# Starting expert 0 of a mixture of experts inside the routing that feeds it

## The chip, the cores and the metric

The kernel runs on one core of a Trainium2 chip. The metric is the device time of one launch, in microseconds (us); lower is better. Engines are named as in the profile: PE (TensorE matmul), PEld (its weight loads), DVE (VectorE), ACT (ScalarE), POOL (GpSimd) and SP (SyncE); the q after a name is that engine's queue of instructions.

## What is computed

A graph attention network of two layers on 1250 nodes of 768 features, then a transformer block: attention over the 1250 rows, and a mixture of experts with 8 experts, of which each row uses 2. The change concerns the last part, in the reference:

```python
logits = xf @ Wrouter                                   # (1250, 768) @ (768, 8)
topk_w, topk_idx = jax.lax.top_k(logits, 2)
topk_w = softmax(topk_w)
we = zeros((N, E)).at[arange(N)[:, None], topk_idx].add(topk_w)
...
h = gelu(xf @ W1e)                                      # 768 -> 384, for each expert e
acc = acc + we_e[:, None] * (h @ W2e)                   # 384 -> 768
```

and the block returns x + attention + that sum, where xf is the layer norm of x + attention. Everything is in 32-bit floats.

## The kernel before

Rows are worked on in 10 row tiles of T = 125 rows. `product(t)` (line 878) multiplies a row tile of the attention result by the output projection (`po`, 12 matmuls of 384 columns, 24 rows in the profile[...]), adds the residual and normalises twice (lines 886 to 892), and sends x + attention to `out` in DRAM from SP or ACT (line 893). The normalised rows are `yn`, one of three buffers.

`route(t, yn, seen)` (line 896) transposes yn on PE (`ptr`, line 140), evicts it through ACT with the norm's scale and bias (`fT`, line 146), multiplies by the router (`pl`, line 901, 8 columns), takes the two largest logits and their indices on DVE, makes one-hot rows `oh`, and counts on PE how many earlier rows chose the same expert (`prk`, lines 918 and 920; `seen` carries the counts of earlier tiles). That count is the row's place among its expert's rows; the slot is 1280 times the expert plus the place (line 939). The two softmax weights are computed with Exp and a reciprocal (lines 927 to 934). Two indirect DMAs from POOL then scatter the row, with four words behind its 768 (row number, first expert, the two weights; RW = 772), into the DRAM table `xd` (line 941). The loop of lines 952 to 957 issues product(t + 1) ahead of route(t); within each engine a scheduler orders the instructions.

After the last tile, `pn` (line 961) counts the rows of each expert over all tiles. From it DVE finds which experts have more than CAP = 384 rows (`used`, `more`, lines 963 to 966) and where the first spare tile is (`pick`, lines 825 to 834). Every engine loads `more` into a register, SP loads the place as well, and a loop (line 1050) runs for each further spare tile; with the given inputs it runs zero times. At the end of such a loop all engines and DMA queues meet.

Experts are worked on as a list of `jobs` (line 1061): expert 0 to 7 with 384 slots, that is three slot tiles of 128 rows, and one spare tile. For each job, `fetch` reads slot tiles from `xd` on SP (`xr`, line 988), `turn` transposes them on PE (`pt`, 6 times 3 transposes) and evicts them through ACT (`xT`), `first` (line 1019) is 18 matmuls (`phe`, 36 rows in the profile) with Gelu on ACT (`hT`), `second` (line 1029) is 6 matmuls for each slot tile (`poe`, 12 rows in the profile), whose result DVE weighs and adds to what the row has so far (`sofar`). `tokens` (line 991) makes the ids and weights on DVE, `results` (line 1003) gathers `sofar` from `out`, and `second` scatters it back; gathers and scatters are indirect DMAs from POOL, ordered job after job because two experts can share a row. The weights of the next expert, `we`, are loaded by SP into one of two buffers while the present one runs, ahead of the next rows; those of expert 0, `first_w`, are loaded early in routing.

The order of the DMAs that SP issues once the loop is passed is: expert 0's three tiles of xr, expert 1's two weight matrices, its three tiles, expert 2's weights, and so on:

```python
xr = fetch(xd[0:CAP, :], NS)
...
over = nc.values_load(more[0:1, 0:1], min_val=0, max_val=NE * NR)
with tc.For_i(0, over, 1):
```

Of the kernel before, what the change touches and what calls it, by code (L numbers as in the profile page):

```python
# [27 lines left out]
def gnn_ffn_kernel(  # L28
# [49 lines left out]
    RW = D + 4  # L78
# [786 lines left out]

    with tc.tile_pool(name="proj", bufs=3, reuse_waits="tile") as pp, \
            tc.tile_pool(name="ppo", bufs=2, space=PSUM) as ppo, \
# [5 lines left out]

        normed = [pp.tile([P, RW], F32, tag=f"yn{i}", name=f"yn{i}", bufs=1) for i in range(3)]
# [3 lines left out]
        def product(t):  # L878
            po = ppo.tile([T, 2, 512], F32, tag="po", name="po")
            for s in range(2):  # L880
                for c in range(DC):
                    nc.tensor.matmul(po[:, s, :DH], aT[:, c, t * T:(t + 1) * T],  # L882
                                     wp[:, c, s * DH:(s + 1) * DH],
                                     start=(c == 0), stop=(c == DC - 1))
            y2 = pp.tile([T, D], F32, tag="y2", name="y2")
            ln_apply(y2, xs[:, t, :], st0[:, 0, t:t + 1], st0[:, 1, t:t + 1])
            o = y2.rearrange("p (s d) -> p s d", s=2)
            nc.vector.tensor_tensor(o, o, po[:, :, :DH], ALU.add)
            mean, rstd = ln_stats(y2)
            yn = normed[t % len(normed)]  # L890
            ln_apply(yn[:T, :D], y2, mean, rstd)
            nc.vector.tensor_add(xs[:, t, :], xs[:, t, :], y2)
            split_rows(nc.sync if t % 2 == 0 else nc.scalar, out[t * T:(t + 1) * T, :], xs[:, t, :])
            return yn

        def route(t, yn, seen):
            fT = pp.tile([P, DC, T], F32, tag="fT", name="fT", bufs=2)
            transpose_rows(ppt, yn[:T, :D], affine(fT, 0, 2))
            pl = ppl.tile([P, 512], F32, tag="pl", name="pl")
            for c in range(DC):  # L900
                nc.tensor.matmul(pl[:T, :NE], fT[:, c, :], wr[:, c, :],
                                 start=(c == 0), stop=(c == DC - 1))
            lg = small.tile([T, NE], F32, tag="lg", name="lg")
# [12 lines left out]
            nc.vector.tensor_add(both, oh[:, 0, :], oh[:, 1, :])  # L916
            pr = ppl.tile([P, 512], F32, tag="pl", name="prk")
# [8 lines left out]

            ex = small.tile([T, 2], F32, tag="ex", name="ex")
            nc.vector.tensor_sub(ex[:, 0:1], top[:, 1:2], top[:, 0:1])
            nc.scalar.activation(ex[:, 0:1], ex[:, 0:1], AF.Exp)
            nc.vector.tensor_scalar(ex[:, 1:2], ex[:, 0:1], 1.0, None, ALU.add)  # L930
            nc.vector.tensor_copy(yn[:T, D:D + 1], number[:, t:t + 1])
            nc.vector.tensor_copy(yn[:T, D + 1:D + 2], atf[:, 0:1])
            nc.vector.reciprocal(yn[:T, D + 2:D + 3], ex[:, 1:2])
            nc.vector.tensor_mul(yn[:T, D + 3:D + 4], ex[:, 0:1], yn[:T, D + 2:D + 3])
# [10 lines left out]
            return new  # L945
# [6 lines left out]
        yns = [product(0)]  # L952
        seen = None
        for t in range(NT):
            if t + 1 < NT:
                yns.append(product(t + 1))
            seen = route(t, yns[t], seen)
# [17 lines left out]
    with tc.tile_pool(name="moe", bufs=2, reuse_waits="tile") as mp, \  # L975
# [15 lines left out]
        def tokens(xr, e, n, tag):  # L991

            ids = mp.tile([P, NS], I32, tag=tag + "ids", name="ids")
            nc.vector.tensor_copy(ids[:, :n], xr[:, :n, D])
            weight = mp.tile([P, NS], F32, tag=tag + "weight", name="weight")
            part = mp.tile([P, NS], F32, tag=tag + "part", name="part")
            nc.vector.tensor_sub(part[:, :n], xr[:, :n, D + 2], xr[:, :n, D + 3])
            nc.vector.scalar_tensor_tensor(part[:, :n], xr[:, :n, D + 1], e, part[:, :n],
                                           op0=ALU.is_equal, op1=ALU.mult)
            nc.vector.tensor_add(weight[:, :n], part[:, :n], xr[:, :n, D + 3])  # L1000
            return ids, weight

        def results(ids, s, row):
            nc.gpsimd.indirect_dma_start(
                out=row, out_offset=None, in_=out,
                in_offset=bass.IndirectOffsetOnAxis(ap=ids[:, s:s + 1], axis=0),
                bounds_check=N - 1, oob_is_err=False)

        def turn(xr, n):
            xT = mp.tile([P, DC, CAP], F32, tag="xT", name="xT")  # L1010
            for c in range(DC):
                pt = mpt.tile([P, 512], F32, tag="pt", name="pt")
                for s in range(n):
                    nc.tensor.transpose(pt[:, s * P:(s + 1) * P], xr[:, s, c * P:(c + 1) * P], ident)
                nc.scalar.activation(xT[:, c, :n * P], pt[:, :n * P], AF.Identity,
                                     scale=lnp[:, 2, c:c + 1], bias=lnp[:, 3, c:c + 1])
            return xT

        def first(w1, xT, n):
            hT = mp.tile([P, FC, CAP], F32, tag="hT", name="hT")  # L1020
            for f in range(FC):
                ph = mph.tile([P, 512], F32, tag="ph", name="phe")
                for c in range(DC):
                    nc.tensor.matmul(ph[:, :n * P], w1[:, c, f * P:(f + 1) * P], xT[:, c, :n * P],  # L1024
                                     start=(c == 0), stop=(c == DC - 1))
                nc.scalar.activation(hT[:, f, :n * P], ph[:, :n * P], AF.Gelu)
            return hT

        def second(w2, hT, s, ids, weight, row):
            po = mpo.tile([P, 2, 512], F32, tag="po", name="poe")  # L1030
            for d in range(2):
                for f in range(FC):
                    nc.tensor.matmul(po[:, d, :DH], hT[:, f, s * P:(s + 1) * P],  # L1033
                                     w2[:, f, d * DH:(d + 1) * DH],
                                     start=(f == 0), stop=(f == FC - 1))
            o = row.rearrange("p (s d) -> p s d", s=2)
            nc.vector.scalar_tensor_tensor(o, po[:, :, :DH], weight[:, s:s + 1], o, op0=ALU.mult, op1=ALU.add)  # L1037
            nc.gpsimd.indirect_dma_start(
                out=out, out_offset=bass.IndirectOffsetOnAxis(ap=ids[:, s:s + 1], axis=0),
                in_=row, in_offset=None, bounds_check=N - 1, oob_is_err=False)  # L1040

        xr = fetch(xd[0:CAP, :], NS)
# [7 lines left out]
        with tc.For_i(0, over, 1):  # L1050
# [5 lines left out]
            ids, weight = tokens(xo, picked[:, EXTRA, 0:1], 1, "o")  # L1056
            results(ids, 0, sofar[0])
            second(w2, first(w1, turn(xo, 1), 1), 0, ids, weight, sofar[0])

        extra = [place(i) for i in range(EXTRA)]  # L1060
        jobs = [(float(e), NS, expert(e), lambda e=e: xd[e * REG:e * REG + CAP, :]) for e in range(NE)]
        jobs += [(picked[:, i, 0:1], 1, chosen(e), lambda r=r: xd[ds(r, P), :])
                 for i, (e, r) in enumerate(extra)]
        xT = turn(xr, NS)
        for i, (e, n, _, _) in enumerate(jobs):
            w1, w2 = w
            hT = first(w1, xT, n)
            ids, weight = tokens(xr, e, n, "")
# [3 lines left out]
            if i + 1 < len(jobs):  # L1072
# [3 lines left out]
                xT = turn(xr, m)  # L1076
# [33 lines left out]
```

## Time and profile before

| | us |
|---|---|
| median of 3 runs | 1528.72 |
| lowest and highest | 1525.68, 1529.65 |
| time of the profiled run | 1527.86 |
| its span, first to last instruction | 1526.1 |
| mean granted clock of PE | 0.961 |
| PE busy | 1442.0 (94%) |
| DVE, ACT, POOL busy | 813.5, 598.0, 433.7 |

By stage, from the windows of the trace (busy us of each engine, and the granted clock of PE as a share of full speed):

| stage | from, to | PE | DVE | ACT | POOL | PE clock |
|---|---|---|---|---|---|---|
| graph, attention | 0, 1184 | 1125.2 | 711.8 | 502.7 | 356.3 | 0.72 to 1.00 |
| projection and routing | 1184, 1276 | 92.0 | 61.3 | 41.0 | 22.7 | 1.00 |
| hand-over to the experts | 1276, 1300 | 8.6 | 9.6 | 8.9 | 3.9 | 0.62 |
| expert 0, into expert 1 | 1300, 1346 | 43.6 | 5.0 | 11.9 | 9.2 | 0.90 |
| experts | 1346, 1526 | 172.6 | 25.9 | 33.4 | 41.6 | 0.99 |

A busy share says how long an engine had work in flight; a stage's length is set by the engine or wait that the chain runs through. In a list of instructions, the bracket after a row is the idle time before it on its engine and what ended it. A tile's name stands for its buffers.

### The profile page before, as it was taken

The page shows a single profiled execution, that of the slowest core. Times are in us where ns is not written, and L with a number is a line of the kernel's source. Part 1 is how long each engine was busy: PE and PEld are TensorE (multiplying, and loading weights), DVE is VectorE, ACT ScalarE, POOL GpSimd, SP SyncE. Part 2 cuts the span into 40 slices and gives each one's busy share as a digit, 9 for nine tenths or more (in the row PEclk, how much of TensorE's full clock was granted, in tenths as well). Part 3 has the DMA queues.
Part 4 walks back from the last instruction along what each step waited for, and adds up shares of the span by engine and source line. Part 5 has one row for each costly group of instructions (what it writes and reads, how often), then busy time and mean ns, then how long its engine had stood idle before and what let it go on. Part 6 is the DMA issues. An engine that isn't in the chain of part 4 may idle for free.

```text
span 1526.1 us, 15935 instructions
## 1 busy us (share of the span) xinstructions
PE 1442.0 (94%) x5957; PEld 781.8 (51%) x5957; DVE 813.5 (53%) x1326; ACT 598.0 (39%) x949; POOL 433.7 (28%) x288
## 2 busy tenths in 40 slices
PE   5699999999999999999999999999989996899998
PEld 3476655556555555553343343344333664566665
DVE  4797655435036650128778778778787764111111
ACT  3321613205116521236646646646656344221211
POOL 6300000000000010006646656655657222122222
PEclk9856999999999999999999999999999997899999
DMA  7100010000031129920000000000120433855644
GB/s 216 33 2 12 11 73 0 1 19 14 0 103 41 61 82 395 407 100 1 21 0 1 21 1 21 1 21 1 29 73 1 143 112 113 299 169 174 223 152 143
DMA packets 48848, 125.50 MB, mean 82 GB/s; under 512 B 6103, under 2 KB 22680, under 8 KB 48768
## 3 DMA queue, kind: packets, MB, share of 16 engines
q1 hardware_dynamic: 30958, 55.99, 11.0%
q0 software_dynamic: 12688, 57.10, 10.0%
q10 hardware_dynamic: 5122, 11.36, 2.6%
q8 instruction: 48, 0.79, 0.2%
q14 instruction: 32, 0.26, 0.1%
HBM read 71.30 MB, written 57.60 MB: 84 GB/s over the span
## 4 chain that ended last, share of the span: by engine, by line
PE 71%; DVE 9%; issue 8%; DMA 6%; ACT 4%; POOL 1%; POOLq 0%; SPq 0%; ACTq 0%; DVEq 0%
PE pagg L542 12%; PE ph L209 9%; PE st L694 8%; PE pav L738 7%; PE pk L657 5%; PE pv L673 5%; PE phe L1024 5%; PE poe L1033 5%; PE pq L657 4%; PE pc L419 2%; DMA xd<-yn,slot 2%; DVE sT L724 2%; PE po L882 2%; ACT sT L697 1%; DVE most L703 1%
## 5 line engine op out<-in xcount | busy, mean ns | idle before, releaser
L730 POOL TENSOR_TENSOR acc<-acc,sT 125x834 f32<-125x834 f32 (+1 forms) x139 | 273.0, 1964 | 10.9
L542 PE MATMUL pagg<-h,wt 125*125 125x385 f32 (+1 forms) x800 | 263.5, 486 | 0.4 <-DVE wt L535 0.4
L703 DVE TENSOR_TENSOR most<-most,st 125x834 f32<-125x834 f32 (+1 forms) x144 | 147.0, 1021 | 107.2 <-ACT sT L697 103.4
L542 PEld LDWEIGHTS pagg<-h,wt 125*125 125x125 f32 x800 | 147.1, 187 | 104.6 <-DVE wt L535 3.5
L724 DVE TENSOR_TENSOR sT<-sT,mb 125x834 f32<-125x834 f32 (+1 forms) x180 | 174.2, 1016 | 22.6 <-PE mb L719 22.6
L725 ACT ACTIVATE sT<-sT 125x834 f32<-125x834 f32 (+1 forms) x180 | 158.4, 900 | 49.3 <-DVE sT L724 49.0
L697 ACT COPY sT<-st 125x834 f32<-125x834 f32 (+1 forms) x180 | 151.5, 848 | 53.2 <-PE st L694 51.2
L694 PE MATMUL st<-qk 64*125 64x417 f32 (+1 forms) x720 | 164.9, 558 | 4.3 <-DVE most L703 4.2
L738 PE MATMUL pav<-sT,v 125*64 125x417 f32 (+1 forms) x720 | 151.8, 534 | 9.5 <-ACT sT L725 9.5
L635 POOL MEMSET zero<- 128x772 f32 x1 | 0.7, 741 | 505.9 <-PE ptr L140 505.9
L730 POOL TENSOR_TENSOR acc<-sT 125x834 f32<-125x834 f32 (+1 forms) x18 | 35.3, 1962 | 277.0 <-ACT sT L725 277.0
L694 PEld LDWEIGHTS st<-qk 64*125 64x125 f32 x720 | 56.9, 185 | 99.7 <-issue 43.2
L738 PEld LDWEIGHTS pav<-sT,v 125*64 125x64 f32 x720 | 42.8, 137 | 106.3 <-issue 43.8
L1033 PE MATMUL poe<-we,hT 128*128 128x384 f32 x264 | 88.8, 486 | 0.0
L657 PE MATMUL pq<-yT,wqk 128*128 128x417 f32 (+1 forms) x216 | 88.1, 534 | 0.0
L1037 DVE SCALAR_TENSOR_TENSOR sofar<-poe,weight,sofar 128x768 f32<-128x768 f32 x25 | 25.4, 1017 | 117.0 <-PE poe L1033 109.4
L882 PE MATMUL po<-wp,aT 128*125 128x384 f32 x240 | 87.5, 498 | 0.0
L209 PE MATMUL ph<-gw,xnT 128*125 128x384 f32 x240 | 85.5, 517 | 2.1 <-DVE cnt L454 2.1
L1024 PE MATMUL phe<-xT,we 128*128 128x384 f32 (+1 forms) x288 | 86.6, 460 | 0.0
L657 PE MATMUL pk<-yT,wqk 128*128 128x417 f32 (+1 forms) x216 | 84.0, 526 | 0.0
L673 PE MATMUL pv<-wv,yT 128*125 128x384 f32 x240 | 79.9, 490 | 1.4 <-issue 1.4
L546 DVE RECIPROCAL rz<-pagg 125x1 f32<-125x1 f32 x20 | 3.3, 166 | 141.5 <-PE pagg L542 141.5
(224 smaller groups left out, 1813.4 us busy)
## 6 DMA issues: line engine op xcount, KB each, us to landing
xd<-zero POOLq DMA_DIRECT2D x8, 3860.0 KB, 47.1
we<-in_L_ffn_W_dram SPq DMA_DIRECT2D x16, 1152.0 KB
xr<-xd SPq DMA_DIRECT2D x25, 386.0 KB
gw<-in_L_gnn_W_dram SPq DMA_DIRECT2D x2, 2304.0 KB
wqk<-in_L_ffn_Wqkv_dram SPq DMA_DIRECT2D x12, 384.0 KB
xres<-in_x_dram SPq DMA_DIRECT2D x10, 375.0 KB
xsd<-xres ACTq DMA_DIRECT2D x10, 375.0 KB
wv<-in_L_ffn_Wqkv_dram SPq DMA_DIRECT2D x1, 2304.0 KB
```

What stands on the lines that cost most here:

```text
L209: nc.tensor.matmul(po[:, s, :DH], xT[:, c, t * T:(t + 1) * T], w[:, c, s * DH:(s + 1) * DH], start=(c == 0), stop=(c == DC - 1))
L542: nc.tensor.matmul(po[:, s, :DH + s], ws[j][:, (d - d0) * T:(d - d0 + 1) * T], h[:, j, s * DH:(s + 1) * DH + s], start=(j == 0), stop=(j = ...
L657: nc.tensor.matmul(pq[:, :w], wqk[:, c, i, :], yT[:, c, c0:c0 + w], start=(c == 0), stop=(c == DC - 1))
L694: nc.tensor.matmul(st[:T, i, :w], self.qk[r, 1, j * T:(j + 1) * T], self.qk[r, 0, self.c0:self.c0 + w], start=True, stop=True)
L697: nc.scalar.copy(s[:, :, :w], st[:T, :, :w])
L703: nc.vector.tensor_tensor(self.most[:, :, :w], prev[:, :, :w], st[:T, :, :w], ALU.max)
L724: nc.vector.tensor_tensor(s[:, :, :w], s[:, :, :w], self.mb[:T, :, :w], ALU.subtract)
L725: nc.scalar.activation(s[:, :, :w], s[:, :, :w], AF.Exp)
L730: nc.gpsimd.tensor_tensor(self.acc[:, :, :w], prev[:, :, :w], s[:, :, :w], ALU.add)
L738: nc.tensor.matmul(self.pav[r, :w], v[:, j, hd0:hd0 + HD], s[:, i, :w], start=(j == 0), stop=(j == NT - 1))
L1024: nc.tensor.matmul(ph[:, :n * P], w1[:, c, f * P:(f + 1) * P], xT[:, c, :n * P], start=(c == 0), stop=(c == DC - 1))
L1033: nc.tensor.matmul(po[:, d, :DH], hT[:, f, s * P:(s + 1) * P], w2[:, f, d * DH:(d + 1) * DH], start=(f == 0), stop=(f == FC - 1))
```

## The change

The two weights are no longer computed in routing. A slot row carries the difference of the two largest logits ("lead") in one word, so RW is 771, and `tokens` forms the weight of a row as 0.5 plus or minus half of tanh(lead / 2), which is the same softmax. Exp, its sum, reciprocal and product leave `route`; one Tanh on ACT and three small DVE operations stand in `tokens`.

Expert 0's first two slot tiles, SOON = 2, are fixed once WITH = 7 row tiles are routed: a matmul (`pfirst`) counts expert 0's rows, and if there are fewer than 256, `lift` raises the count so that later rows start at place 256 (unfilled slots hold zeros and a row number out of range). The two tiles are then fetched into `xr0` on SP, behind the scatters of the first seven row tiles, and a generator `early` runs turn, first, tokens, results and second on them. `product`, `route`, `turn` and `first` become generators that yield between groups of matmuls. From product 9 on, PE's order is written out by hand with `go`: product 9 with route 7 in between, then the transposes of xr0 behind those of tile 8, the three f-steps of `first` between the steps of routes 8 and 9, and the two `second` at the end. `pn` and what follows from it come behind that. Expert 0's job in the expert stage has one slot tile, rows 256 to 383, and in the new order of SP its fetch stands ahead of the loop's branch. `turn`, `first`, `tokens`, `results` and `second` are moved up and take their pools as arguments.

```diff
     NR = (REG - CAP) // P
-    RW = D + 4
+    RW = D + 3
+    SOON = 2
+    WITH = 7
...
+    def turn(xr, n, pool, psum, tag):
+
+        xT = pool.tile([P, DC, n * P], F32, tag="xT", name="xT")
+        for c in range(DC):
+            pt = psum.tile([P, 512], F32, tag=tag, name="pt")
+            for s in range(n):
+                nc.tensor.transpose(pt[:, s * P:(s + 1) * P], xr[:, s, c * P:(c + 1) * P], ident)
+            nc.scalar.activation(xT[:, c, :], pt[:, :n * P], AF.Identity,
+                                 scale=lnp[:, 2, c:c + 1], bias=lnp[:, 3, c:c + 1])
+            yield xT
+
...
+    def tokens(xr, e, n, pool, tag):
+
+        ids = pool.tile([P, n], I32, tag=tag + "ids", name="ids")
+        nc.vector.tensor_copy(ids, xr[:, :n, D])
+
+        lead = pool.tile([P, n], F32, tag=tag + "lead", name="lead")
+        pin(nc.scalar.activation(lead, xr[:, :n, D + 2], AF.Tanh, scale=0.5))
+        weight = pool.tile([P, n], F32, tag=tag + "weight", name="weight")
+        nc.vector.tensor_scalar(weight, xr[:, :n, D + 1], e, -0.5, ALU.is_equal, ALU.add)
+        nc.vector.tensor_mul(weight, weight, lead)
+        nc.vector.tensor_scalar(weight, weight, 0.5, None, ALU.add)
+        return ids, weight
+
...
+            tc.tile_pool(name="soon", bufs=1, reuse_waits="tile") as sp, \
...
+        soon = [sp.tile([P, D], F32, name=f"soon{s}") for s in range(SOON)]
+        for r in soon:
+            nc.gpsimd.memset(r, 0.0)
...
+            nc.vector.tensor_copy(yn[:T, D:D + 1], number[:, t:t + 1])
+            yield yn
+
+        def route(t, yn, tally):
+
             fT = pp.tile([P, DC, T], F32, tag="fT", name="fT", bufs=2)
             transpose_rows(ppt, yn[:T, :D], affine(fT, 0, 2))
+            yield None
             pl = ppl.tile([P, 512], F32, tag="pl", name="pl")
             for c in range(DC):
                 nc.tensor.matmul(pl[:T, :NE], fT[:, c, :], wr[:, c, :],
                                  start=(c == 0), stop=(c == DC - 1))
+            yield None
...
-            ex = small.tile([T, 2], F32, tag="ex", name="ex")
-            nc.vector.tensor_sub(ex[:, 0:1], top[:, 1:2], top[:, 0:1])
-            nc.scalar.activation(ex[:, 0:1], ex[:, 0:1], AF.Exp)
-            nc.vector.tensor_scalar(ex[:, 1:2], ex[:, 0:1], 1.0, None, ALU.add)
-            nc.vector.tensor_copy(yn[:T, D:D + 1], number[:, t:t + 1])
+            tally.append(new)
+            yield None
             nc.vector.tensor_copy(yn[:T, D + 1:D + 2], atf[:, 0:1])
-            nc.vector.reciprocal(yn[:T, D + 2:D + 3], ex[:, 1:2])
-            nc.vector.tensor_mul(yn[:T, D + 3:D + 4], ex[:, 0:1], yn[:T, D + 2:D + 3])
+            nc.vector.tensor_sub(yn[:T, D + 2:D + 3], top[:, 0:1], top[:, 1:2])
             rank = small.tile([T, 2], F32, tag="rank", name="rank")
             for i in range(2):
                 nc.vector.scalar_tensor_tensor(oh[:, i, :], oh[:, i, :], 1.0, pr[:T, :NE],
...
+        def early(w1, w2):
+
+            for xT in turn(xr0, SOON, sp, ppt, "tr"):
+                yield None
+            for hT in first(w1, xT, SOON, sp, ppl, "pl"):
+                yield None
+            ids, weight = tokens(xr0, 0.0, SOON, sp, "")
+            for s in range(SOON):
+                results(ids, s, soon[s])
+            for s in range(SOON):
+                second(w2, hT, s, ids, weight, soon[s], ppo)
+                yield None
+
+        def go(steps, n=1):
+            for _ in range(n):
+                r = next(steps)
+            return r
+
+        yns = [last(product(0))]
+        tally = [None]
+        for t in range(NT - 3):
+            yns.append(last(product(t + 1)))
+            last(route(t, yns[t], tally))
+            if t == WITH - 1:
+
+                pn = ppl.tile([P, 512], F32, tag="pl", name="pfirst")
+                seen = tally[-1]
+                nc.tensor.matmul(pn[:, :NE], ones, seen, start=True, stop=True)
+                lift = small.tile([1, 1], F32, tag="lift", name="lift")
+                nc.vector.tensor_scalar(lift, pn[0:1, 0:1], -1.0, float(SOON * P), ALU.mult, ALU.add)
+                nc.vector.scalar_tensor_tensor(seen[0:1, 0:1], lift, 0.0, seen[0:1, 0:1], op0=ALU.max, op1=ALU.add)
+                xr0 = sp.tile([P, SOON, RW], F32, name="xr0")
+                for s in range(SOON):
+                    ins = nc.sync.dma_start(xr0[:, s, :], xd[s * P:(s + 1) * P, :])
+                    tc.add_to_no_dep_group("slots", ins.ins)
+        assert WITH == NT - 3
+        yns.append(last(product(NT - 2)))
+        with tc.manual_schedule(engines={mybir.EngineType.PE}):
+            a, b = route(NT - 3, yns[NT - 3], tally), product(NT - 1)
+            go(b, 3)
+            go(a)
+            go(b, 2)
+            go(a)
+            go(b, 4)
+            go(a, 2)
+            go(b, 3)
+            yns.append(go(b))
+            x = early(*w)
+            a, b = (route(t, yns[t], tally) for t in (NT - 2, NT - 1))
+            go(a)
+            go(x, DC)
+            go(a)
+            go(b)
+            go(x)
+            go(a, 2)
+            go(b)
+            go(x)
+            go(b, 2)
+            go(x)
+            seen = tally[-1]
+            go(x, SOON)
...
-        xr = fetch(xd[0:CAP, :], NS)
+        xr = fetch(xd[SOON * P:CAP, :], NS - SOON)
...
-        jobs = [(float(e), NS, expert(e), lambda e=e: xd[e * REG:e * REG + CAP, :]) for e in range(NE)]
+        jobs = [(0.0, NS - SOON, None, None)]
+        jobs += [(float(e), NS, expert(e), lambda e=e: xd[e * REG:e * REG + CAP, :]) for e in range(1, NE)]
...
-        xT = turn(xr, NS)
+        xT = last(turn(xr, NS - SOON, mp, mpt, "pt"))
```

## The prediction

> **What bounds the kernel now.** I read the 40 slices of the page first, then the chain of waits from 1180 us on, then one-microsecond windows over the place where TensorE goes quiet, then the instructions there one by one. Times inside the span are profile microseconds.
>
> The slices:
>
> ```profile
> PE   5699999999999999999999999999989996899998
> PEclk9856999999999999999999999999999997899999
> ```
>
> TensorE is at 9 tenths nearly everywhere; the late hole is one slice of 6 with clock 7. The chain shows what the hole is:
>
> ```profile
> 1184.50 12.45 PE po L882 x38
> ...
> 1266.82 28.60 DMA xd<-yn,slot x2
> ...
> 1297.37 5.78 DMA xr<-xd
> ...
> 1309.47 10.32 PE phe L1024 x32
> ...
> 1333.68 11.61 PE phe L1024 x36
> 1345.29 0.66 PE pt L1014 x6
> ```
>
> Three stages: projection and routing, where TensorE never waits (its row of the windows is full from 1184 to 1275); a hand-over, in which the last scatters land, everything meets at the overflow loop, and expert 0's rows are fetched; then the experts, again TensorE without a gap, 25.5 us each (phe at 1333.68, 1359.18, 1384.68). So the time is set by when `first` of expert 1 ends: 1345.29. Whatever moves that moment moves the end; after it the two kernels do the same TensorE work.
>
> The hand-over in windows (columns: stretch, length, busy of PE, PEld, DVE, ACT, POOL, then granted clock, DMA share, GB/s):
>
> ```profile
> 1276.00:1277.00 1.00, 0.71 (x6) 0.43 (x4) 0.96 (x2) 0.93 (x3) 0.00 (x0) 1.00 0.74 293
> 1279.00:1280.00 1.00, 0.00 (x0) 0.00 (x0) 0.93 (x8) 1.00 (x1) 0.00 (x0) 1.00 0.62 175
> 1281.00:1282.00 1.00, 0.00 (x0) 0.00 (x0) 0.93 (x7) 0.99 (x2) 0.00 (x0) 0.83 0.00 0
> 1308.00:1309.00 1.00, 1.00 (x3) 0.29 (x3) 0.00 (x0) 0.61 (x1) 0.00 (x0) 0.51 1.07 440
> ```
>
> The clock halves at 1281.8, 6.1 us after the last wide matmul (1275.65), and is whole again at 1309. The instructions that set the hand-over:
>
> ```profile
> 1265.52 0.95 DVE L888 TENSOR_TENSOR y<-y,po 125x768 f32<-125x768 f32 x1 [2.48 <-PE po L882]
> 1266.39 0.15 DVE L934 TENSOR_TENSOR yn<-ex,yn 125x1 f32<-125x1 f32 x1
> 1266.82 0.98 POOL L941 DMA_INDIRECT xd<-yn,slot  x1 [10.92 <-DVE yn L934]
> ...
> 1283.66 2.69 PE L901 MATMUL pl<-wr,fT 128*125 128x8 f32 x12
> ...
> 1289.35 0.22 DVE L963 SCALAR_TENSOR_TENSOR used<-pn,used 128x56 f32<-128x56 f32 x1 [0.17 <-PE pn L961]
> ...
> 1291.32 0.14 DVE L833 CAST index<-picked 1x1 int32<-1x1 f32 x1
> ...
> 1315.05 0.17 DVE L994 CAST ids<-xr 128x3 int32<-128x3 f32 x1 [11.14 <-DMA xr<-xd]
> ```
>
> The last line: expert 1's rows land only at 1315, since weights and rows queue behind each other at 380 to 420 GB/s.
>
> **What the Trainium skill says.** "TensorE: Matmul & The Clock Gate", Part 1: the clock is released after about a 3.4 us window of matmul activity and taken after an idle one, windows running freely; Part 4: transposes do not count as busy in the same way. The trace agrees with the first: clock changes at 1281.8 and 1309.0 lie 8 x 3.4 us apart. For transposes it shows that a window with only them, 1.3 us of 3.4, loses the clock (at 46.0 us). "ScalarE: Activation LUTs", What ACT_TABLE_LOAD costs: a set switch costs 1.28 us plus a drain; the load takes 1.28 us here too.
>
> **The change, part by part.** Sums are made against the profiled run (span 1526.1, timed 1527.9, 0.9 below the median 1528.7); I add only the difference to the median.
>
> *Removed from routing:* Exp with its two table loads per tile (2.6 us of ACT) and four small DVE operations of about 0.15 us. TensorE covers these up to 1275, so nothing there. One effect matters: slots of tile 6 are ready at 1262.0, but its scatters wait for line 934, queued behind a wait for po, until 1266.4. Without it they leave at about 1262.5 and 1263.8 and land by 1268 (3.1 to 4.4 us each). The rows of xr0, fetched on SP (3.5 and 4.1 us from issue to use for the first two tiles of xr), are there by 1272.
>
> *xr0 as a new wait.* DVE's conversion of its ids stands inside tile 7's routing, behind max_index, at about 1272; behind it queue tile 7's one-hots, and behind those on TensorE the rank matmul and the last half of product 9. Cover: just enough, 0 to 1 us. SP's out write of tile 8 behind xr0 has until 1269 and is waited for by nobody soon. POOL has the two gathers ahead of tile 8's scatters; they wait for the out write of tile 9 (about 1283), earlier than those slots. Nothing.
>
> *TensorE's new order*, from the end of product 9 (1275.65, plus 0.3 for the extra count matmul and 0.6 for tile 7's pl, no longer mixed with po): 1276.6. Transposes of tile 8, 0.8: 1277.4. Then 12 transposes of xr0, paced by ACT: 2.2 us of fT, four evictions of 256 columns (0.52 each, between 0.36 at 125 and 0.67 at 384), the square root 0.3 and two DMA issues 0.65 ahead of the last pair: 1283.0. No wide matmul since 1276.6, so I take the clock as halved. pl of tile 8 at half clock 2.7 (row above): 1285.7; transposes of tile 9 1.5 (as at 1282.17): 1287.2. The first phe of 12 rows: 256/384 of 0.3225 is 0.215 us a row, 0.43 at half clock, recovering towards its end, 4.5: 1291.7. Rank of tile 8, its two DVE reads (pl reuses that PSUM buffer), pl of tile 9 and its copy: 2.4: 1294.1. phe 2.6, rank 0.5, phe 2.7: 1299.9. poe 24 rows of 0.327: 1307.8; pn 0.3: 1308.1. Before, pn ended at 1289.3.
>
> *After pn.* DVE first does the second early tile's sum (1.02), so `used` starts at 1309.0; 2.1 to the index (1289.35 to 1291.46), 1.9 for SP's register loads (1291.5 to the branch at 1293.4): fetch at 1313.0. The third tile takes 3.5, and the loop's meeting waits for it, 0.5: TensorE starts at T = 1317.0, against 1300.0 before. Scatters of tile 9 (landing near 1304) and of the early tiles (near 1313) end sooner.
>
> *Expert 0 with one tile.* 6 transposes and the first phe paced by ACT 3.5, other phe rows mostly at half clock 5.9 (the last job's 36 rows took 4.18 at full), poe's first half 2.0: T + 11.4. Then expert 1's rows: 2.36 MB of weights, 1.18 of rows, 0.4 of gather and some of expert 2's weights at 0.385 MB/us, 1.7 to start: T + 13. With poe's other half and the first transposes, T + 13.8; twelve more transposes 1.4, 36 phe rows 11.6, eviction waits 1.2: `first` of expert 1 ends at T + 28 = 1345.0. Before: 1345.29. The two tiles that leave the expert stage are paid back by a start 17 us later: **a gain of 0.3, 1528.4 us.**
>
> *Unknowns, both ends.* xr0's wait: 0 to +5 (row times shift to before's 1268.1). Clock in the early tiles: -4.3 (never lost: pl 1.6, transposes 0.7, phe 2.0) to +5.2 (lost through all three phe, 2.6 each for two more). Third tile's landing: -0.5 to +1. Expert 1's rows: -1 to +2; they only bind if late. Rows of 771 words, not 772: 0.13% fewer bytes, the odd stride unseen; -0.2 to +1, I take 0, as scatters and fetches other than the first are covered. Tanh and Gelu follow each other with no table load between in the built order: 0; if ACT had to switch, 1.3 an expert, hidden. The correction of ranks: seven tiles send 269 tokens to expert 0 (counted from the inputs with the reference), above 256, so it adds nothing; expert 6's 419 needs the one spare tile in both, and the loop body stays unused.
>
> **Rivals.** *Faster, 1523.9:* the clock holds through the early tiles, since transposes add activity; pn ends at 1303.8, `first` at 1340.7, 4.6 less. For: a window with 0.8 us of wide matmul and 0.9 of transposes kept it (59.7 to 63.1). Against: 7.9 us without wide matmuls holds a whole window wherever it falls; before lost it in such a stretch. It could also come from faster fetches. *Slower, 1533.6:* the clock stays halved through all three phe, because pl and rank matmuls of 8 columns and their DVE round trips stand between them: 2.6 twice, 5.2 on everything behind. It decides if the gap between the first and second phe exceeds 2.4 us. For: tiny matmuls at 74 to 130 us, dense, never released the clock. Against: the first phe alone is 5.1 us long at half clock, longer than a window. *Late xr0, 1532:* 1 us past the cover is 1 us lost; scatters at before's place would cost 4. A part of the slower side. *The change doesn't do what it says:* excluded by the built order.
>
> **How the numbers follow.** About 0.3% (4.6 us) is what a measurement can tell from no change. Forecast case 0.50; faster 0.28; slower, the late xr0 included, 0.22. The range 1522 to 1533.5 takes in the clock both ways, and leaves out 1 in 10 on each side; the likeliest case's own is 1525 to 1531.5.
>
> **What would show it.** Right: xr0's ids near 1272; a halved clock at the first phe; pn near 1308; TensorE starting expert 0's last tile near 1317; expert 1's `first` ending near 1345. Wrong: pn before 1304, or a start less than 8 us after pn (faster); clock 0.5 at the second phe, or DVE stopped at ids past 1274 (slower).

## The result, and the profile after

The changed kernel takes 1525.76 us (median of 20 runs, 1520.93 to 1529.55); beside them the kernel before took 1529.55 us (20 runs, 1525.68 to 1532.43). The ratio is 0.9977, 95% interval 0.997 to 0.9985: a gain of 3.5 us, between 2.3 and 4.6. It lies inside the 0.3% that was called no change beforehand, but it is not zero. The two profiled executions, 1527.86 and 1525.74 us, differ by 2.1 only, since that of before lay 1.7 under its median. What these two traces can account for is therefore 2.1 us; the rest of the 3.5 has no place in them. Three executions of the later comparisons took 1.87 to 3.68 ms, far from all others, and stand outside the ratios.

The slices of the page after:

```profile
PE   5699999999999999999999999999988999799998
PEclk9756999999999999999999999999999998899999
```

Where before there was a slice of 6 with the clock at 7 and behind it one of 8 with the clock at 8, there is one of 9 and one of 7, both with the clock at 8: TensorE works where it stood still, and part of that work is done slowly. The chain of waits after (start, length, what):

```profile
1185.06 12.45 PE po L947 x38
...
1282.30 1.81 PE pl L970 x12
...
1285.45 4.69 PE phe L885 x12
...
1292.62 4.56 PE phe L885 x12
...
1297.64 2.86 PE phe L885 x12
1300.49 7.75 PE poe L918 x24
1308.27 1.02 DVE soon L922
...
1312.90 3.41 DMA xr<-xd
...
1317.90 10.20 DMA xr<-xd
...
1334.44 10.32 PE phe L885 x32
1344.77 0.65 PE pt L874 x6
```

The first line is the start of routing, at 1184.50 before; the last marks the end of `first` of expert 1, at 1345.29 before. Three first products of the early tiles lie between, equal in work; they take 4.69, 4.56 and 2.86 us. The windows show why (the columns are those of the windows of before; the clock is the third number from the right):

```profile
1282.00:1283.00 1.00, 1.00 (x10) 1.00 (x9) 0.00 (x0) 0.90 (x2) 0.00 (x0) 0.87 0.09 34
1283.00:1284.00 1.00, 1.00 (x7) 1.00 (x6) 0.00 (x0) 0.00 (x0) 0.37 (x1) 0.50 0.00 0
1289.00:1290.00 1.00, 1.00 (x5) 0.77 (x5) 0.00 (x0) 0.00 (x0) 0.00 (x0) 0.72 0.00 0
...
1292.00:1293.00 1.00, 0.74 (x6) 0.63 (x6) 0.53 (x5) 0.00 (x0) 0.69 (x2) 0.99 0.23 93
1293.00:1294.00 1.00, 1.00 (x4) 0.82 (x3) 0.93 (x8) 0.00 (x0) 0.57 (x1) 0.50 0.72 275
...
1296.00:1297.00 1.00, 1.00 (x6) 0.83 (x4) 0.00 (x0) 0.00 (x0) 0.00 (x0) 0.80 0.00 0
```

A window of one microsecond with clock 0.87 was at half clock for 0.26 us, so the clock fell at 1282.74; in the same way it came back at 1289.56, fell again at 1292.98 and came back at 1296.40. Two falls in this stretch, not the one of the forecast; a third, at 1313.46, comes in the wait ahead of the loop. The first four times are 6.82, 3.42 and 3.42 us apart. "TensorE: Matmul & The Clock Gate", Part 1, of the Trainium skill states free-running windows of 3.413 us, and this grid agrees with it: in each of the thirteen profiles kept here the changes of the clock between 1255 and 1345 us lie whole multiples of 3.41 us apart, to about 0.01 us.

Two instructions of the timeline answer to the forecast's waits. One is the conversion of the early ids on VectorE, which waits for nothing; the other is TensorE's first instruction behind the loop, 8.84 us after its last:

```profile
1272.41 0.16 DVE L898 CAST ids<-xr 128x2 int32<-128x2 f32 x1
```

```profile
1317.20 0.69 PE L874 MATMUL pt<-ident,xr 128*128 128x128 f32 x2 [8.84 <-DMA xr<-xd]
```

**Where 2.1 us went.** The routing starts 0.56 us later after than before (work that the change doesn't touch). From there to the end of `first` of expert 1 it is 159.71 us after and 160.79 before: a gain of 1.08. From that point to the end of the span it is 179.23 and 180.81: a gain of 1.58, where none was forecast. This last part has two places. Each expert's step is shorter, as the chains show, before and then after:

```profile
1345.29 0.66 PE pt L1014 x6
1345.94 0.65 PE poe L1033 x2
1346.59 0.40 PE pt L1014 x3
1346.99 0.01 issue
1347.00 0.55 PE pt L1014 x3
...
1348.86 10.32 PE poe L1033 x32
```

```profile
1344.77 0.65 PE pt L874 x6
1345.42 0.65 PE poe L918 x2
1346.07 0.48 PE pt L874 x3
1346.55 0.65 PE poe L918 x2
1347.20 0.66 PE pt L874 x6
...
1348.84 9.68 PE poe L918 x30
```

Before, TensorE does six transposes of the next expert, then a second product, then six, and its second six take 0.96 us with a stop for ScalarE in the middle (0.40, 0.01, 0.55). After, a second product stands at that stop, and the same six take 0.48 and 0.33. From one expert's phe to the next it is 25.36 us (1358.51 to 1383.87) in place of 25.50 (1333.68 to 1359.18). The phe of the last job starts 164.51 us after the mark in place of 165.37: 0.86 gained over six steps. The remaining 0.72 is the tail, in which GpSimd's scatters into the output wait for each other. VectorE's last sum, before and then after:

```profile
1519.50 1.02 DVE L1037 SCALAR_TENSOR_TENSOR sofar<-poe,weight,sofar 128x768 f32<-128x768 f32 x1 [7.62 <-DMA sofar<-out_dram,ids]
```

```profile
1517.40 1.02 DVE L922 SCALAR_TENSOR_TENSOR sofar<-poe,weight,sofar 128x768 f32<-128x768 f32 x1 [3.15 <-PE poe L918]
```

Before, it waits for the last gather, which stands behind the scatters; TensorE's last product had ended 0.78 us earlier. After, it starts 0.06 us behind TensorE's last product. So the 0.86 of the shorter steps counts in full, and the 0.72 is what the scatters had held up before. The first scatter of the last whole expert, before and then after:

```profile
1504.42 4.05 DMA out_dram<-sofar,ids
```

```profile
1503.04 3.09 DMA out_dram<-sofar,ids
```

In the chains of before, after and the experiments most of these scatters take 3.1 us and a few 3.8 to 4.6, not always the same ones, so I count the 0.96 between these two as chance. From the end of `first` of expert 1 to the end of the span it is 179.2 to 180.4 us in the ten profiles with the new weight and 180.1 to 181.1 in the three with the old: the tail alone can move one profile by about a microsecond.

### The profile page after: what moved, and what is told of

Read it like the earlier page. It is cut to its first block, busy times and chain, and to the rows that moved or that the text cites. A ratio compares the mean times of both kernels' runs of the same rounds, so it can differ in the third digit from the quotient of the medians.

```text
span 1524.0 us, 16014 instructions
## 1 busy us (share of the span) xinstructions
PE 1445.9 (95%) x5995; PEld 787.3 (52%) x5995; DVE 810.5 (53%) x1302; ACT 576.9 (38%) x940; POOL 433.2 (28%) x290
## 4 chain that ended last, share of the span: by engine, by line
PE 74%; DVE 10%; issue 5%; DMA 5%; ACT 5%; POOL 1%; SPq 0%; POOLq 0%; ACTq 0%; DVEq 0%
PE pagg L544 13%; PE ph L211 9%; PE st L696 8%; PE pav L740 7%; PE po L947 5%; PE pk L659 5%; PE pv L675 5%; PE pq L659 4%; PE phe L885 4%; PE poe L918 4%; PE pc L421 2%; DVE sT L726 2%; ACT sT L699 2%; PE ptr L142 1%; DVE most L705 1%
## 5 line engine op out<-in xcount | busy, mean ns | idle before, releaser
L732 POOL TENSOR_TENSOR acc<-acc,sT 125x834 f32<-125x834 f32 (+1 forms) x139 | 273.0, 1964 | 10.9
L211 PE MATMUL ph<-gw,x1T 128*125 128x384 f32 x240 | 78.5, 487 | 0.0
```

What stands on the lines that cost most here:

```text
L211: nc.tensor.matmul(po[:, s, :DH], xT[:, c, t * T:(t + 1) * T], w[:, c, s * DH:(s + 1) * DH], start=(c == 0), stop=(c == DC - 1))
L732: nc.gpsimd.tensor_tensor(self.acc[:, :, :w], prev[:, :, :w], s[:, :, :w], ALU.add)
```

## The experiments

Three questions are open: which part of the change gains (the lead in the rows, or the early tiles), what the two falls of the clock cost and what brings them, and what the meeting of the engines ahead of the loop waits for. Times of the stretches are counted from the start of the routing's first product in the same trace, because that start itself lies between 1182.1 and 1189.1 us in the profiles of these kernels (one each), whose work on TensorE up to there is the same. Each kernel was measured beside the kernel before; a difference "of ratio" is that of two such ratios, times 1529 us. The forecasts name the count of tokens, which is the matmul `pn`; its time is that of its start.

**The lead alone.** The kernel before with

```diff
-    RW = D + 4
+    RW = D + 3
...
-            nc.scalar.activation(ex[:, 0:1], ex[:, 0:1], AF.Exp)
...
-            nc.vector.reciprocal(yn[:T, D + 2:D + 3], ex[:, 1:2])
+            nc.vector.tensor_sub(yn[:T, D + 2:D + 3], top[:, 0:1], top[:, 1:2])
...
+            pin(nc.scalar.activation(lead[:, :n], xr[:, :n, D + 2], AF.Tanh, scale=0.5))
```

> The kernel before with one part of the change alone: rows of 771 values that carry the first term's lead, the weight from a Tanh, and no early tiles. If the change gains in the experts' steps because the new weight's instructions let the transposes be ordered in the other way between the second products (theory), a step from the end of one expert's first products to the next takes 25.36 us in place of 25.50, over seven steps about 0.9 us, the hand-over from routing to expert 1 stays at the length of before, and the time is 1 to 1.5 us under before (ratio 0.999 to 0.9995). If the early tiles gain all of it (rival), steps stay at 25.50 and the ratio is 1.000; if the lead gains all of it (second rival), the ratio is near 0.9977.

1527.94 us, before 1528.50 beside it; ratio 0.9991 (0.9982 to 1.0001). The chain has the steps of the changed kernel:

```profile
1336.33 11.61 PE phe L1019 x36
...
1352.01 9.68 PE poe L1028 x30
1361.69 11.61 PE phe L1019 x36
```

25.36 us. So the shorter step comes from the new weight's instructions, not from the early tiles: with them the order of TensorE is built as in the changed kernel. The gain expected from it, 0.9 us, is too small for the interval to tell from nothing; that the step is 0.14 us shorter, the trace shows. In this profile VectorE's last sum waited for a gather until 1.06 us after TensorE's last product, so the shorter steps didn't reach the end in full. From the routing's start to the end of `first` of expert 1 it was 161.4 us, no shorter than before's 160.9.

**The early tiles alone.** The changed kernel with the rows and weights of before:

```diff
-    RW = D + 3
+    RW = D + 4
...
+            nc.scalar.activation(ex[:, 0:1], ex[:, 0:1], AF.Exp)
...
-            nc.vector.tensor_sub(yn[:T, D + 2:D + 3], top[:, 0:1], top[:, 1:2])
+            nc.vector.reciprocal(yn[:T, D + 2:D + 3], ex[:, 1:2])
```

> The changed kernel with the old weights: rows of 772 values, Exp and reciprocal in the routing, early tiles kept. Theory: steps of 25.50 us as before; the routing of tile 6 writes its rows later, by the Exp's round trip over ScalarE, so that the ids of the early rows wait on VectorE to about 1275 and hold product 9 and the last routing by 0 to 4 us; the time is 1 to 4 us over the changed kernel (ratio to before 0.9985 to 1.001). Rival: the old weights cost nothing and the early tiles gain all of it, the ratio to before stays near 0.9977 with no wait for the early rows.

1530.13 us; ratio 1.0008 (1.0 to 1.0016), 4.7 us of ratio above the changed kernel. Steps of 25.51 us. The timelines of GpSimd and of VectorE:

```profile
1267.68 0.98 POOL L1011 DMA_INDIRECT xd<-yn,slot  x1 [11.11 <-DVE yn L1004]
```

```profile
1277.43 0.25 DVE L898 CAST ids<-xr 128x2 int32<-128x2 f32 x1 [1.00 <-DMA xr<-xd]
```

Tile 6's rows leave at 1267.68 and not at 1263.16, the early rows' ids are read 5 us later and now wait for their fetch; the count stands at 126.3 us from the routing's start in place of 123.1. Without the lead the early tiles lose, if anything. The two halves of the change are not two gains: by the ratios the lead alone is worth 0.9 thousandths, the early tiles alone cost 0.8, and both together gain 2.3. The lead's chief use is that it lets the early rows be written in time.

**The count first.**

```diff
             seen = tally[-1]
+            pn = ppl.tile([P, 512], F32, tag="pl", name="pn")
+            nc.tensor.matmul(pn[:, :NE], ones, seen, start=True, stop=True)
...
+                pick(-1.0e9 if i == 0 else picked[:, i - 1, 1:2], i)
...
             go(x, SOON)
...
-        pn = ppl.tile([P, 512], F32, tag="pl", name="pn")
...
```

> The changed kernel with the last count (pn) and the pick of the extra tile ahead of the two second products of the early tiles on TensorE, and VectorE in the same order. Theory (the meeting of the engines ahead of the loop waits for the pick and the fetch of expert 1's rows and tokens): the pick ends about 5 us earlier, the fetch of tokens starts at about 1303 and not 1312.9, and the meeting then waits for the early results' scatter, at about 1313 to 1314 in place of 1317; first products of expert 1 end near 1341 to 1342, the time is about 3 us under the changed kernel (ratio to before 0.9955). Rival: the last fetch isn't what the meeting waits for, or expert 1's weights and rows come at the same time anyway: no difference (0.9977).

1523.31 us; ratio 0.996 (0.9945 to 0.9974), 2.6 us of ratio under the changed kernel. The chain in front of the loop:

```profile
1307.09 0.98 DMA out_dram<-soon,ids
1308.07 2.66 issue
...
1310.96 3.19 DMA out_dram<-soon,ids
```

The fetch was issued at 1304.93, and the last thing to arrive is now the scatter of the second early result, at 1314.15, as expected. TensorE starts 129.5 us from the routing's start, in the changed kernel 132.2. So in the changed kernel it is the count behind the second products, the pick and the fetch that hold the meeting.

**Filling matmuls.** Eight matmuls of 128x256 into a PSUM tile that nobody reads, six between the early transposes and two in the gap between the first and the second early phe:

```diff
+            def fill(c):
+                nc.tensor.matmul(idle[:T, 0, :256], aT[:, c, :T], wp[:, c, :256], start=True, stop=True)
...
-            go(x, DC)
+            for c in range(DC):
+                fill(c)
+                go(x)
...
             go(a, 2)
+            fill(0)
             go(b)
+            fill(1)
             go(x)
```

> The changed kernel with eight matmuls of 128x256 that nobody reads, one between each pair of early transposes, one after the rank product of tile 8 and one after the router product of tile 9, so that TensorE has wide work where its clock fell. Theory (clock): the granted clock stays up through the three first products of the early tiles, each about 2.5 us in place of 4.9, 4.5 and 2.9, the count ends 3 to 5 us earlier than 1308, less about 1.5 us for the added matmuls; the time is 2 to 3.5 us under the changed kernel (ratio to before 0.9955 to 0.9965). Rival: the clock falls as before for want of enough work, or the routing chain on the other engines sets the end of this stretch: the time is the changed kernel's or up to 2 us over it (0.9977 to 0.999).

1520.59 us; ratio 0.994 (0.9925 to 0.9955), more than expected. The clock is 1.00 in every window from 1264 to 1294; the three phe take 2.60, 2.60 and 2.86 us and the count stands at 118.3 us. Extra work on the busiest engine made the kernel faster, by 5.7 us of ratio against the changed one (5.2 by the medians; `first` of expert 1 ends 4.8 us earlier by the traces).

**Only the two in the gap, only the six between transposes.**

The edit of the filled kernel with one of its two halves left out:

```diff
+            fill(0)
             go(b)
+            fill(1)
```

> The changed kernel with only the two filling matmuls that lie in the gap between the first and the second first product of the early tiles. Theory (two separate falls of the clock, the second owed to the 2.5 us gap with little wide work): the first product of early block 0 stays at about 4.9 us with half the clock, block 1 takes 2.6 to 2.9 us in place of 4.5; less 0.4 to 0.8 us of added work, the count ends about 1 us earlier than in the changed kernel, counted from the start of the routing (122 us in place of 123.1). Rival (the second fall follows from the first, or comes at a time of its own whatever lies in the gap): block 1 stays at 4.5 us and the count ends 0.5 us later.

```diff
-            go(x, DC)
+            for c in range(DC):
+                fill(c)
+                go(x)
```

> The changed kernel with only the six filling matmuls between the early transposes. Theory (the first fall is owed to the 4 us in which TensorE has but transposes and waits): block 0 takes 2.6 us in place of 4.9, the router product and the transposes of tile 9 run at full clock as well (1.2 and 0.7 us in place of 2.0 and 1.5), about 3.5 us gained less up to 1 us of added work; in the gap the second fall may come as in the changed kernel (4.5 us). Count at about 120.5 us from the start of the routing, in place of 123.1. Rival: the clock falls at block 0 all the same, no gain.

With the two in the gap: 1524.85 us, ratio 0.9977 (0.9969 to 0.9985), the same as the changed kernel. With the six: 1521.40 us, ratio 0.996 (0.9946 to 0.9973). TensorE's timeline of the second:

```profile
1284.94 2.76 PE L885 MATMUL phe<-xT,first_w 128*128 128x256 f32 x12
...
1288.48 1.45 PE L970 MATMUL pl<-wr,fT 128*125 128x8 f32 x12 [0.44 <-DVE oh L1003]
1290.18 2.86 PE L885 MATMUL phe<-xT,first_w 128*128 128x256 f32 x12 [0.26 <-DVE lg L974]
```

With six fills there is no fall in this stretch, though the gap (1287.54 to 1290.18) is as thin as before, and the count stands at 118.3 us, as with all eight: by the traces the two in the gap were not needed (the intervals of the ratios overlap and don't tell). With the two alone, the second phe took 2.75 us, as the theory had it, and the count stood at 122.2 us, also as it had it. But the theory isn't shown by that. Half clock lasted 10.2 us there (1277.88 to 1288.12, by the windows) and 6.8 + 3.4 us in the changed kernel: as much in all, in one piece that began earlier. In both profiles the first fall comes in the thin stretch behind product 9, but 5.9 us after its last wide matmul in the changed kernel and 3.3 us after it here.

Whether the second fall comes depends also on where the windows lie; the gap alone doesn't bring it. The windows can be counted on from each profile's own falls in steps of 3.41 us. In the changed kernel the gap (1290.14 to 1292.62) lies whole in one window (1289.56 to 1292.98), and the clock falls at that window's end; so it is, to 0.06 us, with the early tiles alone and with the count first. With six fills the next fall is at 1306.78:

```profile
1306.00:1307.00 1.00, 0.00 (x0) 0.89 0.00 0
```

Five steps back is 1289.71, inside the gap: each of the two windows holds over a microsecond of wide matmuls, and neither loses the clock. With the two fills alone the gap (1288.72 to 1291.31) again lies whole in one window (1288.12 to 1291.53), and no fall comes: there the two fills held the clock, in this one profile. The first fall is another matter. Without the six fills no wide matmul runs for 8.4 us (1276.81 to 1285.25), more than two windows, so one whole window always lies in that stretch. All five profiles without the six fills fell there (changed, early tiles alone, count first, early loads, only the gap filled), and none of the five with them did.

**Expert 1's weights loaded ahead of the routing**, into a buffer of their own, first in the kernel before as a control, then in the changed one:

```diff
+    next_w = ahead.tile([P, 2 * DC * FF], F32, name="next_w")
...
         w = load_expert(first_w, *expert(0))
+        w_next = load_expert(next_w, *expert(1))
...
-                w = load_expert(mp.tile([P, 2 * DC * FF], F32, tag="w", name="we"), *ws)
+                w = w_next if i == 0 else load_expert(
+                    mp.tile([P, 2 * DC * FF], F32, tag="w", name="we"), *ws)
```

> The kernel before with expert 1's weights loaded ahead of the routing into a buffer of their own, in place of behind the loop. Control for the next run: in the kernel before TensorE has all three tiles of expert 0 to do (about 28 us) while these loads land, so both theories expect no change: ratio 0.999 to 1.001.

> The changed kernel with expert 1's weights loaded ahead of the routing into a buffer of their own, so that behind the loop only its rows are fetched. Theory (what is left of expert 0 behind the meeting is too short to hide 3.5 MB): the rows land some 5 us earlier, the 0.6 us wait of the transposes for them goes and with it up to 0.5 us of waits on ScalarE, 0.6 to 1.2 us under the changed kernel. Rival (the early tiles lose most of their gain to these loads): 3 us or more under it. Second rival: nothing.

The control: 1528.01 us beside 1529.43, ratio 0.9993 (0.9982 to 1.0004), no change. In the changed kernel 1524.75 us, ratio 0.9964 (0.995 to 0.9979), 2 us of ratio under it where 0.6 to 1.2 was expected; the intervals overlap. The stop for the rows is gone from TensorE's timeline, but this profile also shows a single fall of the clock ahead of the count (1285.08 to 1291.90) with nothing added in the gap:

```profile
1285.00:1286.00 1.00, 0.61 (x4) 0.54 0.98 286
...
1291.00:1292.00 1.00, 1.00 (x4) 0.55 0.77 148
```

Its first phe took 3.6 us and its second 2.9, which I don't put down to the weights. Up to the early transposes TensorE's times, counted from the routing's start, are those of the changed kernel to 0.01 us; only the windows lie elsewhere, and one ends inside the gap (at 1295.31; the gap is 1293.77 to 1296.26). The count stands at 120.9 us and not 123.1. `first` of expert 1 ends 5.3 us earlier than in the changed kernel; 2.2 of it is this, and 1.3 more is the clock in the first products of expert 0's last tile (4.12 us in place of 5.42). That leaves at most 1.8 us for the weights in these two profiles, an estimate; the size of what early loads alone bring stays open.

**Filling and counting first; then with early loads.** The diffs are those above, two of them in the first kernel and three in the second.

> Both of the earlier edits on the changed kernel, filling matmuls and the count ahead of the early second products. Theory (the meeting waits for the count, the pick and a fetch; with the count first it waits for the scatter of the second early result): the two gains come from different steps, so they add for the most part: about 3.5 us under the filled kernel, ratio to before 0.991 to 0.992. Rival (they remove the same wait): no more than 1 us under the filled kernel, 0.9935 to 0.994.

> The three edits together on the changed kernel: filling matmuls, the count first, and expert 1's weights loaded ahead of the routing. Theory: with a clock that stays up the wait of expert 1's transposes for their rows is about 2 us (it was 1.9 in the filled kernel), and early loads take it away: 1.5 to 2.5 us under the kernel with two edits, ratio to before 0.989 to 0.9905. Rival: the rows are then held by the fetch behind the meeting itself, no gain over two edits.

Both edits: 1520.13 us, ratio 0.9943 (0.9931 to 0.9956), the number of the rival. The trace says otherwise: TensorE starts behind the loop at 124.8 us from the routing's start, in the filled kernel at 127.3, and `first` of expert 1 ends 2.7 us earlier. The two profiled executions, 1518.16 and 1517.61 us, differ by 0.55 only, since the routing of the filled kernel's started 2.0 us earlier, and each lies about 2.5 us under its median. So whether the two edits add stays open. All three: 1516.38 us, ratio 0.992 (0.9908 to 0.9932), the fastest version: 12 us under the kernel before, 8.7 us of ratio under the changed one. Its chain has no transfer left behind the loop:

```profile
1303.84 3.41 DMA out_dram<-soon,ids
...
1312.12 5.34 PE phe L887 x32
1317.47 0.66 PE pt L876 x6
...
1323.56 11.61 PE phe L887 x36
```

Expert 1's transposes follow at once; in the filled kernel they waited 1.94 us for their rows.

**Filling the wait ahead of the loop too**, eight more matmuls behind the early second products of the kernel with three edits:

```diff
             go(x, SOON)
+            rest = ppo.tile([P, 2, 512], F32, tag="po", name="idle")
+            for _ in range(8):
+                nc.tensor.matmul(rest[:T, 0, :256], before, xs[:, 0, :256], start=True, stop=True)
```

> The kernel with all three edits and eight more filling matmuls of 128x256 in the wait ahead of the loop. Theory (the 6.5 us idle stretch of TensorE ahead of the loop costs the clock in expert 0's last tile, whose first products took 5.5 us there and 4.1 us in the run with early loads alone): first products near 4.1 us, 1 to 1.5 us under the kernel with three edits, ratio to before near 0.991. Rival: the fall comes all the same, since more than 3 us of the wait stay empty, no gain.

1517.12 us, ratio 0.9928 (0.9914 to 0.9941): no gain, the rival's number. The windows of that kernel (TensorE's busy time, then the clock):

```profile
1308.00:1310.00 2.00, 0.43 (x3) 1.00 0.42 162
1310.00:1312.00 2.00, 0.69 (x2) 0.72 0.23 32
1312.00:1314.00 2.00, 1.90 (x8) 0.50 0.95 313
```

The fills ended at 1308.4, and with the 2.6 us still empty behind them the clock fell at 1310.87, before TensorE's next instruction (1311.07). By the trace `first` of expert 1 ends 0.4 us earlier than without these fills, too little to tell.

| kernel | count, from the routing's start | end of `first` of expert 1, from there | ratio to before, 95% |
|---|---|---|---|
| before | 104.3 us | 160.9 us | 1 |
| changed | 123.1 | 159.8 | 0.9977 (0.997 to 0.9985) |
| lead alone | 104.9 | 161.4 | 0.9991 (0.9982 to 1.0001) |
| early tiles alone | 126.3 | 162.3 | 1.0008 (1.0 to 1.0016) |
| count first | 115.3 | 157.0 | 0.996 (0.9945 to 0.9974) |
| filled | 118.3 | 155.0 | 0.994 (0.9925 to 0.9955) |
| six fills only | 118.3 | 155.3 | 0.996 (0.9946 to 0.9973) |
| two fills only | 122.2 | 159.1 | 0.9977 (0.9969 to 0.9985) |
| early loads in the kernel before | 104.3 | 161.1 | 0.9993 (0.9982 to 1.0004) |
| early loads in the changed kernel | 120.9 | 154.5 | 0.9964 (0.995 to 0.9979) |
| filled, count first | 110.5 | 152.3 | 0.9943 (0.9931 to 0.9956) |
| filled, count first, early loads | 110.5 | 151.3 | 0.992 (0.9908 to 0.9932) |
| the same, the wait filled too | 110.5 | 150.9 | 0.9928 (0.9914 to 0.9941) |

## Why the prediction came out as it did

No change was called, at 1528.4 us; it became 1525.76, inside the range, with a gain that is real and small, but 3.5 us where the sum gave 0.3. Step by step:

**The early rows.** Forecast: ids near 1272, no stall. Measured: 1272.41, no stall; and the experiment without the lead shows the 5 us by which they would have been late. The cost of lateness was put at 4 us. By the traces it was 3.2 us at the count and 2.6 at the end of `first` of expert 1; by the ratios it was 4.7, of which up to 0.9 belongs to the expert steps. Right in kind, and near in size.

**The early tiles' stretch.** The sum said that pn would end at 1308.1 for a routing that starts at 1184.5, which is 123.6 us; it ended at 123.4. That is luck in part: it came out right by errors against each other. The second phe was put at 2.6 us and took 4.56, since the clock fell a second time (2.0 too little). Against that, the router product of tile 8 took 1.81 where 2.7 was put, as the clock was still whole at its start, the stretch from product 9 to the end of the early transposes took 5.5 (1276.81 to 1282.30) where 6.4 was put, and smaller terms made up the rest. The slower rival's mechanism was partly there: its second phe at half clock, which the forecast had named as a sign of that case, and not its third. Its criterion, a gap of over 2.4 us, was met (2.48 us), but the later runs show that the gap alone doesn't decide: the windows of early loads gave this order one fall and not two. One reading was slightly off, and nothing hangs on it: before, the clock fell at 1281.67 by the window's 0.83, not at 1281.8.

**The meeting and expert 0's last tile.** T was put at 1317.0, 132.5 us from the routing's start; it was 132.2. `first` of expert 1 was put at T + 28.0; it took 27.6. Together they give a gain of 1.1 us where 0.3 was forecast; the term of 28 us, with its rows landing at T + 13 (the first landed at T + 10.9, the last at T + 13.0), was 0.4 too large. That is as near as the working allows.

**The step that failed** is the sentence that after the end of `first` of expert 1 "the two kernels do the same TensorE work". They do the same work in another order: 0.14 us less an expert step, 0.86 us over six of them. The order of TensorE is fixed when the kernel is built; I compared it around the change and took the experts behind it as equal. The kernel with the lead alone shows that this belongs to the Tanh weight, which the forecast had put at 0. The unchanged tail gave another 0.72 us, by one scatter that landed in 3.1 us and not 4.1, which no step could foresee. Both together are the 1.6 us of the traces' difference that the forecast didn't have.

**Not placed.** The medians differ by 3.8 us and the profiles by 2.1. The routing's start alone moves by several microseconds from profile to profile, and where the windows lie moved the count by 2.2 us in the same order of TensorE. Two traces don't settle where the other 1.7 lies.

## What to carry to other kernels

Work that is moved into a hole of the busiest engine is paid at the clock that the hole leaves behind. Here the stretch from the meeting to the end of `first` of expert 1 became 17.7 us shorter (45.3 to 27.6) and the meeting came 16.6 later, with 10.2 us of the way at half clock; a few filling matmuls in the thin stretch gained about 5 us where the whole move had gained 3.5. Where engines meet (here ahead of a loop that runs no times), ask what arrives last, and put the short chain that feeds it ahead of long work that nobody waits for. When a change touches an instruction that is used everywhere, compare the built order everywhere, and not at the change alone: a tenth of a microsecond in a repeated step was as large as the effect that was studied.

## What was unexpected in the hardware

Six matmuls of 128x256 (0.43 us each, some 2.6 us in 5.1) among twelve transposes kept the clock whole in five profiles of five. Transposes, the narrow products of routing and waits alone lost it in five of five, 3.3 to 5.9 us after the last wide matmul.

"TensorE: Matmul & The Clock Gate", Part 1, warns that the phase of the free-running windows makes cold counts vary. Here the same phase decides whether a stretch of routing has one fall of 6.8 us or two of 6.8 and 3.4 (early loads, 1285.08 to 1291.90, and the changed kernel); with two fills in the gap there was one of 10.2 us (1277.88 to 1288.12). So two profiles with the same order of TensorE can differ by 2 us.
